# A third attention that makes its scores twice, with the shift put into the queries between

## The chip, the cores and the metric

One core of a Trainium2 chip runs the whole kernel. The metric is the device time of one execution in microseconds; the kernel before takes 1277.92 us, the median of 3 runs (1277.36 to 1278.59). The core's engines are TensorE (PE, with its weight loads as PEld), VectorE (DVE), ScalarE (ACT), GpSimd (POOL) and SyncE (SP, which issues most DMAs). TensorE writes only to PSUM, which here is eight banks of 128 x 512 floats.

## The reference

Everything is float32, for 4 batches of 256 tokens of width 256 and a context `ctx` of the same size. Four layers follow each other:

- L0: two cross attentions to the context (16 heads of 128, one learned key each), and an MLP.
- L1: layer norm, attention of `x` to `ctx` (16 heads of 16, keys masked per batch), MLP.
- L2: attention to the context and `x` together (512 keys, 16 heads of 16, keys masked), MLP.
- L3: grouped-query attention, 32 query heads on 8 key heads of 8, with a full additive mask per batch, then layer norm:

```
scores = einsum("bkgld,bksd->bkgls", q, k) / sqrt(8)
scores = scores + mask                # mask: (B, 1, 256, 256)
attn   = softmax(scores, axis=-1)
out    = einsum("bkgls,bksd->bkgld", attn, v)
y      = layer_norm(out @ Wo + bo + hidden)
```

## The kernel before

The kernel is a list of `Task` objects (L173). A task may have TensorE work (`run`) of one of three shapes, "full" (the whole array), "rows" (contraction of 32, four row groups side by side) and "cols" (32 output columns, four column groups), and posts: work for VectorE, ScalarE, GpSimd or SP once the TensorE work is done. A `Post` that names two engines leaves the choice to the planner. Tiles come from rings: `takes` waits for a free tile, `gives` returns it. `PS` is the ring of eight PSUM banks, `EE` holds weights and MLP activations, `QK` queries and keys, `EQ` (8 tiles) scores and saved sums, `M3` the third attention's mask.

The order of the work is written out by hand as a list of task numbers, `ORDER` (L1841). `plan` (L1754) walks it with a cost for every task and post, picks each free post's engine, and the kernel is issued in that order; every engine then works strictly in its order. A tuple in `ORDER` is two "rows" tasks of different `pair` (row groups 0, 1 and 2, 3) issued interleaved, so that four matmuls run at once; a "rows" task alone keeps half of the row groups idle for the same time. `pe` and `turn` (transpose, a matmul with the identity) and all engine calls pass through `Pinned` (L126), which is why the profile shows L134 nearly everywhere.

The batches go through the layers after L0 one after the other, but the order mixes them: while one is in an MLP, another is in an attention. Before about 700 us only L0 runs.

The third attention (`attention`, L364, with key 3) fetches the mask by SP, makes queries (four copies, one for each group of heads, the rest of the 32 rows zeroed) and keys, and then runs `unit8` (L579) twice per batch, for 16 heads each. For each of four head groups `j`, and for two pairs, `scores` makes 256 x 256 scores with queries in partitions; `least` (VectorE) adds the mask, negates, writes the sum to an `eq` tile and its minimum to `nm`; `exps` (ScalarE) takes the exponential with `nm` as bias; `turns` (TensorE) transposes the weights, since the product with the values needs keys in partitions; the copy to an `e` tile is VectorE's or ScalarE's; `weighted` multiplies with the values, which carry a column of ones for the sum. `ending` (L525) turns the result, divides, and turns it back. At the end of the layer the projection makes its two halves (`part`, L793) in one PSUM bank, `half` adds each to `X`, and `closing` (L923) normalizes and sends it out.

Attentions one and two (`unit16`, L670) make their scores twice already. First with queries in partitions, only for the maxima, which `most` writes negated into a column of a zeroed `shift` tile; that tile is turned (one tile for each of two head groups) and added to the queries, in rows that no head uses (`SHIFT`), opposite a row of ones in the keys. The second scores come out with keys in partitions and less their maxima, so ScalarE takes the exponential straight from PSUM with no turn behind it. Their mask goes with the key and so into the keys (`plus`) or the bias. `open_late` (L1619) makes the tiles of these layers when L0 is done.

Of the kernel before, what the change touches and what calls it, by code (L numbers as in the profile page):

```python
# [51 lines left out]
def kernel(ctx: ExitStack, tc: tile.TileContext, a: dict, out: bass.AP):  # L52
# [60 lines left out]
    SHIFT, HIDDEN = (16, 0), (17, 1)  # L113

# [81 lines left out]
    tasks, stage = [], 0  # L196
# [6 lines left out]
    QK, VV, EQ, OT, XO, M3, HIDES, PLUS, RAW = (Ring([]) for _ in range(9))  # L203
    PO = [Ring([None, None]) for _ in range(2)]
    SHIFTS = [Ring([]), Ring([])]
# [114 lines left out]
    class Layer:  # L320
# [17 lines left out]
        def fill(self):  # L338
# [6 lines left out]
            self.bkx = bk if key == 3 else late_tile([P, 2, 2], f"bkx{key}")  # L345
            for g in range(nh):
                if key == 3:
                    ge.tensor_scalar(self.bqx[:, :, g], self.bq, self.selq[:, g : g + 1], None, ALU.mult)
                else:
# [3 lines left out]
                    )  # L353
            if key != 3:
# [5 lines left out]

                self.hide = late_tile([P, B * S // P], f"hide{key}")
                ge.tensor_scalar(self.hide, self.raw, 0.0, HIDE, ALU.is_equal, ALU.mult)

    def attention(L, b, after, hTs, dst, dst_after, weights_at, before):  # L364
# [13 lines left out]
        if key == 3:  # L378
# [3 lines left out]
            masks = Task(b, None, 0, None, before, takes=[(M3, st, "m")], posts=[Post(("SP",), 100, fetch)], lag=4.0)  # L382
        else:
# [34 lines left out]
        def keys(t, after, q, give):  # L418
# [12 lines left out]
            if key == 3:  # L431
                posts = [affine(lambda: q["kx"](), lambda: u["pt"][2][:, :S], None, lambda: L.bkx[:, t : t + 1], gives)]
                return Task(b, "full", 0.864, run, after, takes=[(PS, u, "pt")], posts=posts)
# [65 lines left out]
        qs, with_mask, use_v = [], [], [[] for _ in L.sources]  # L499
        for t in range(2):  # L500
            q = {"shift": {}}
            q["qm"] = lambda q=q: q["qk"][2][:, : nh * S].rearrange("p (g s) -> p g s", g=nh)
            if key == 3:
                q["kx"] = lambda q=q: q["qk"][2][:, nh * S : nh * S + S]
            else:
                q["kx"] = lambda q=q: q["qk"][2][:, nh * S : nh * S + 2 * NK].rearrange("p (g s) -> p g s", g=2)
            qs.append(q)
# [71 lines left out]
        def unit8(t, q):  # L579
            u = {}  # L580
            S_tasks, V_tasks = [], []
            for j in range(4):
                turned, Ss = [], []
                grab = Task(
                    b, None, 0, None, S_tasks or ready[t] + [masks], behind=vs_taken,
                    takes=[(EE, u, j)] + ([(PO[1], u, "pm"), (PS, u, "po")] if j == 0 else []),
                )
                for pair in range(2):
                    v = {}

                    def scores(j=j, pair=pair, v=v):
                        for qt in range(2):
                            for i in range(2):
# [3 lines left out]
                                    q["qm"]()[r, j, qt * P : (qt + 1) * P], q["kx"]()[r, :], True, True,  # L597
# [3 lines left out]
                    def least(e, i, v=v):  # L601

                        v["nm", i] = sm.tile([P, 2], F32, tag="nm3", name="nm3", bufs=10)
                        for qt in range(2):
                            ve.tensor_tensor_reduce(
                                v["eq", i][2][:, qt, :], v[i][2][:, qt * S : (qt + 1) * S], st["m"][2][:, qt, :],
                                -1.0, BIG, ALU.add, ALU.min, accum_out=v["nm", i][:, qt : qt + 1],
                            )

                    takes = [(PS, v, 0), (PS, v, 1), (EQ, v, ("eq", 0)), (EQ, v, ("eq", 1))]  # L610
                    ts = Task(
                        b, "rows", 0.857, scores, [grab], takes=takes, pair=pair,
                        posts=[
                            Post(("DVE",), 690, lambda e, i=i, least=least: least(e, i), gives=[(PS, v, i)])
                            for i in range(2)
                        ],
                    )
                    Ss.append(ts)
                    for i in range(2):
                        def exps(e, i=i, v=v):  # L620
                            for qt in range(2):
                                to = v["eq", i][2][:, qt, :]
                                se.activation(to, to, AF.Exp, bias=v["nm", i][:, qt : qt + 1], scale=-1.0)

                        def turns(i=i, v=v):
                            for kc in range(2):
# [1425 lines left out]
```

## Time and profile before

| | |
|---|---|
| runs | 1277.36, 1277.92, 1278.59 us |
| profiled execution | 1278.34 us; span 1276.4 us, TensorE clock 0.998 |
| TensorE | 1259.7 us busy, 8907 matmul records |
| VectorE, ScalarE, GpSimd | 833.5, 702.2, 348.7 us busy |
| transposes of `eq` tiles | 624 records of 128x128, 512 of them weights of the third attention |
| score matmuls, 32x256 | 1536 records, two to a matmul, 512 of them in the third attention |
| exponentials of `eq` (ScalarE) | 256, 107.8 us |
| first and last of them | start at 1023.8 and 1261.7 us |

In a group's line stand the line, the engine, the operation, out<-in by the program's names, partitions x elements, the count, then busy time and mean duration, then idle time of the engine before it and what ended it. In the table of stretches each row is a window, its length, then busy time and instruction count of PE, PEld, DVE, ACT and POOL, the granted clock, the DMA share and GB/s. A timeline row has start, duration, engine, line, operation, names, shapes and count. A matmul's duration holds its way through the array, so rows overlap; the pitch is the difference of starts.

### The profile page before, as it was taken

The numbers are of one execution on the slowest core, as the hardware profiler recorded it, in microseconds if no ns is written. First come the engines' busy times: TensorE is split into PE (matmuls) and PEld (weight loads), VectorE is DVE, ScalarE is ACT, GpSimd is POOL, SyncE is SP. The second block draws the span as 40 slices with busy tenths as digits, with TensorE's granted clock in tenths as the row PEclk, the third lists the DMA queues.
The fourth block names the chain that finished last, engine by engine and source line by source line (L and its number), as shares of the span: only waits on it lengthen the run. The fifth ranks groups of instructions, "written<-read, shape, count | busy, mean of one in ns | idle before, by whom it ended". The sixth has DMA issues, their size and how long they took to land.

```text
span 1276.4 us, 23614 instructions
## 1 busy us (share of the span) xinstructions
PE 1259.7 (99%) x8907; PEld 1040.6 (82%) x8907; DVE 833.5 (65%) x2312; ACT 702.2 (55%) x1689; POOL 348.7 (27%) x570
## 2 busy tenths in 40 slices
PE   8999999999999999999999999999999999999997
PEld 4888898999898988899899877768677677677775
DVE  4856656566767566566565358585375587668798
ACT  3554544444545545554544345454535686678896
POOL 7831601414334214151123433121120201002001
PEclk9999999999999999999999999999999999999999
DMA  7010010101101002001020411000000000000000
GB/s 246 18 50 2 33 51 22 62 1 33 51 17 42 26 17 67 1 17 34 1 73 7 149 39 52 2 2 10 1 5 2 1 2 10 1 2 2 18 6 22
DMA packets 25633, 38.08 MB, mean 30 GB/s; under 512 B 2244, under 2 KB 16086, under 8 KB 25392
## 3 DMA queue, kind: packets, MB, share of 16 engines
q1 hardware_dynamic: 24640, 35.56, 8.6%
q0 software_dynamic: 608, 0.76, 0.5%
q8 instruction: 70, 1.15, 0.3%
q14 instruction: 43, 0.35, 0.1%
q10 hardware_dynamic: 272, 0.26, 0.1%
HBM read 35.52 MB, written 1.05 MB: 29 GB/s over the span
## 4 chain that ended last, share of the span: by engine, by line
PE 93%; DVE 3%; POOL 1%; issue 1%; DMA 1%; ACT 0%; SPq 0%; DVEq 0%; POOLq 0%
PE ps_pj L134 25%; PE ps_o L134 23%; PE ps_s L134 23%; PE ps_et L134 22%; DMA craw<-in_ctx_dram 1%; DVE E L134 1%; DVE X L134 1%; POOL f L134 0%; POOL sc L134 0%; DVE nm L134 0%; DVE e L134 0%; DVE eq L134 0%; ACT E L134 0%; SPq L134 0%; POOL cT L134 0%
## 5 line engine op out<-in xcount | busy, mean ns | idle before, releaser
L134 ACT ACTIVATE eq<-eq,nm 128x256 f32<-128x256 f32 x256 | 107.8, 507 | 4.4 <-DVE nm L134 4.2
L134 POOL TENSOR_TENSOR sc<-cT 128x256 f32<-128x256 f32 x62 | 45.3, 731 | 229.8 <-ACT cT L134 202.8
L134 DVE TENSOR_SCALAR E<-E,rinv 128x257 f32<-128x257 f32 x256 | 100.6, 456 | 2.3
L134 PE MATMUL ps_o<-qk 32*128 32x256 f32 (+1 forms) x284 | 79.6, 449 | 0.0
L134 PE MATMUL ps_s<-qk 32*128 32x256 f32 (+1 forms) x272 | 76.2, 461 | 0.0
L134 PE MATMUL ps_pj<-qk 32*128 32x256 f32 (+1 forms) x246 | 70.8, 458 | 0.0
L134 POOL TENSOR_TENSOR X<-X,rowbc 128x256 f32<-128x256 f32 x56 | 40.0, 739 | 97.4 <-PE ps_et L134 49.2
L134 PE MATMUL ps_et<-qk 32*128 32x256 f32 (+1 forms) x222 | 64.9, 448 | 0.0
L134 POOL TENSOR_SCALAR mv<-mv 128x2 f32<-128x2 f32 (+1 forms) x32 | 7.2, 225 | 190.2 <-DVE mv L134 190.0
L134 PE MATMUL ps_o<-eq,qk 32*128 32x256 f32 x224 | 52.3, 398 | 0.0
L134 PE MATMUL ps_pj<-eq,qk 32*128 32x256 f32 x196 | 47.7, 398 | 0.0
L134 ACT ACTIVATE E<-ps_s,nm 128x257 f32<-128x257 f32 x69 | 32.7, 476 | 25.6 <-DVE nm L134 25.6
L134 PE MATMUL ps_et<-eq,qk 32*128 32x256 f32 x180 | 44.4, 397 | 0.0
L134 ACT ACTIVATE E<-ps_et,nm 128x257 f32<-128x257 f32 x73 | 34.6, 475 | 17.2 <-DVE nm L134 17.2
L134 PE MATMUL ps_et<-kT,qT 128*128 128x257 f32 x146 | 43.2, 381 | 0.0
L134 DVE TENSOR_REDUCE nm<-ps_et 128x1 f32<-128x257 f32 x73 | 30.6, 420 | 19.2 <-PE ps_et L134 18.4
L134 PEld LDWEIGHTS ps_o<-qk 32*128 32x128 f32 x284 | 38.3, 184 | 5.8 <-issue 2.3
L134 POOL TENSOR_SCALAR plus<-hide_r,rowof,bkx 128x256 f32<-128x256 f32 x32 | 17.6, 554 | 91.6 <-DVE qk L134 91.2
L134 PE MATMUL ps_s<-eq,qk 32*128 32x256 f32 x168 | 42.2, 398 | 0.0
L134 DVE TENSOR_REDUCE shift<-ps_s 128x1 f32<-128x512 f32 (+1 forms) x54 | 36.8, 684 | 7.5 <-PE ps_s L134 2.7
L134 DVE TENSOR_TENSOR X<-ps_pj,X 128x128 f32<-128x128 f32 (+2 forms) x86 | 25.3, 305 | 23.7 <-PE ps_pj L134 22.4
L134 PE MATMUL ps_o<-eT,V 128*128 128x256 f32 x160 | 40.8, 379 | 0.0
(591 smaller groups left out, 4027.4 us busy)
## 6 DMA issues: line engine op xcount, KB each, us to landing
wk<-in_L_xattn_wk_dram SPq DMA_DIRECT2D x8, 512.0 KB, 3.5
wv<-in_L_xattn_wv_dram SPq DMA_DIRECT2D x8, 512.0 KB, 3.8
wq<-in_L_xattn_wq_dram SPq DMA_DIRECT2D x8, 512.0 KB, 5.0
wo<-in_L_xattn_wo_dram SPq DMA_DIRECT2D x8, 512.0 KB, 3.8
bvb<-in_bv_dram SPq DMA_DIRECT2D x8, 256.0 KB, 5.3
bvl<-in_cols_dram SPq DMA_DIRECT2D x8, 256.0 KB, 5.6
f<-in_L_xattn_w_fc_dram SPq DMA_DIRECT2D x2, 1024.0 KB, 5.0
f<-in_L_xattn_mlp_w_dram SPq DMA_DIRECT2D x2, 1024.0 KB, 5.1
```

The source lines that it names most:

```text
L134: return lambda *args, **more: tc.keep_in_program_order(f(*args, **more))
```

## The change

The third attention takes the form of the other two. Its first scores serve only for `least`, which writes the negated maximum of scores plus mask into one column of a shift tile; the masked scores themselves go to a tile that nobody reads. One shift tile serves all four head groups: group `j` uses row `SHIFT8[j]` of each 32, a row that is zero in that group's queries. The keys are kept in two forms, one with ones in rows 24 to 26 (for groups 0 to 2) and one with ones in row 0 (for group 3). The tile is turned once (two transposes), and four `scalar_tensor_tensor` on VectorE put the shift into the queries in place. The second scores come with keys in partitions, for two head groups and one half of the keys at a time. The mask, which depends on query and key, is turned once per batch and added to them: for half of the row groups VectorE adds it from PSUM into the `e` tile; for the other half ScalarE copies the scores there and GpSimd adds the mask in place. ScalarE then takes the exponential in place. The turns of the weights and their copies are gone.

Besides: attentions one and two use one shift tile for both head groups, so one turn, and put the shift into the queries in place instead of a third tile; queries and keys come free after the second scores, not after the last product with the values; `EQ` has 4 tiles; the last projection uses a PSUM bank for each half; `ORDER` is another list, for the new set of tasks, all stages included.

```diff
 SHIFT, HIDDEN = (16, 0), (17, 1)
+SHIFT8 = (24, 25, 26, 0)
...
+        if key == 3:
+            self.ones, self.selk = late_tile([P, 2], "ones3"), late_tile([P, 2], "selk3")
+            r = [rowof[:, c : c + 1] for c in SHIFT8]
+            ge.tensor_tensor(self.ones[:, 0:1], r[0], r[1], ALU.add)
+            ge.tensor_tensor(self.ones[:, 0:1], self.ones[:, 0:1], r[2], ALU.add)
+            ge.tensor_copy(self.ones[:, 1:2], r[3])
+            ge.tensor_scalar(self.selk, self.ones, -1.0, 1.0, ALU.mult, ALU.add)
+            for v in range(2):
+                ge.tensor_scalar(
+                    self.bkx[:, :, v], bk, self.selk[:, v : v + 1], self.ones[:, v : v + 1], ALU.mult, ALU.add
+                )
...
+            self.picks = late_tile([P, 2], f"picks{key}")
+            for g in range(2):
+                ge.tensor_tensor(
+                    self.picks[:, g : g + 1], rowof[:, SHIFT[g] : SHIFT[g] + 1], rowof[:, HIDDEN[g] : HIDDEN[g] + 1],
+                    ALU.add,
+                )
...
+        def turned():
+            for kc in range(2):
+                for qt in range(2):
+                    turn(
+                        um["pt"][2][:, kc * S + qt * P : kc * S + (qt + 1) * P],
+                        st["m"][2][:, qt, kc * P : (kc + 1) * P],
+                    )
+
+        mask_turned = Task(
+            b, "full", 0.436, turned, [masks], takes=[(PS, um, "pt"), (MT, st, "mt")],
+            posts=[
+                copied(
+                    lambda: st["mt"][2].rearrange("p k q -> p (k q)"), lambda: um["pt"][2], 512, [(PS, um, "pt")]
+                )
+            ],
+        )
...
+            posts = [
+                affine(
+                    lambda v=v: q["kx"]()[:, v, :], lambda: u["pt"][2][:, :S], lambda v=v: L.selk[:, v : v + 1],
+                    lambda v=v: L.bkx[:, t, v : v + 1], gives if v else [],
+                )
+                for v in range(2)
+            ]
...
+        u = {"e": {}}
+        Ms = []
+        grab = Task(b, None, 0, None, ready[t] + [masks], takes=[(SHIFT8S, q["shift"], 0)])
         for j in range(4):
...
+                def maxima(j=j, pair=pair, v=v):
                     for qt in range(2):
...
-                def least(e, i, v=v):
-
-                    v["nm", i] = sm.tile([P, 2], F32, tag="nm3", name="nm3", bufs=10)
+                def least(e, i, j=j, pair=pair, v=v):
+                    at = 64 * pair + 32 * i + SHIFT8[j]
                     for qt in range(2):
                         ve.tensor_tensor_reduce(
-                            v["eq", i][2][:, qt, :], v[i][2][:, qt * S : (qt + 1) * S], st["m"][2][:, qt, :],
-                            -1.0, BIG, ALU.add, ALU.min, accum_out=v["nm", i][:, qt : qt + 1],
+                            unread[0], v[i][2][:, qt * S : (qt + 1) * S], st["m"][2][:, qt, :],
+                            -1.0, BIG, ALU.add, ALU.min, accum_out=q["shift"][0][2][:, qt, at : at + 1],
                         )
 
-                takes = [(PS, v, 0), (PS, v, 1), (EQ, v, ("eq", 0)), (EQ, v, ("eq", 1))]
+                Ms.append(
+                    Task(
+                        b, "rows", 0.857, maxima, [grab], takes=[(PS, v, 0), (PS, v, 1)], pair=pair,
+                        posts=[
+                            Post(("DVE",), 690, lambda e, i=i, least=least: least(e, i), gives=[(PS, v, i)])
+                            for i in range(2)
+                        ],
+                    )
+                )
+        used_m.extend(Ms)
+        v = {}
+
+        def turns(v=v):
+            for qt in range(2):
+                turn(v["pt"][2][:, qt * P : (qt + 1) * P], q["shift"][0][2][:, qt, :])
+
+        def shift(e, j, v=v):
+            qm = q["qm"]()[:, j, :]
+            ve.scalar_tensor_tensor(
+                qm, v["pt"][2][:, :S], rowof[:, SHIFT8[j] : SHIFT8[j] + 1], qm, ALU.mult, ALU.add
+            )
+
+        shifted = Task(
+            b, "full", 0.218, turns, Ms, takes=[(PS, v, "pt")],
+            posts=[
+                Post(("DVE",), 400, lambda e, j=j: shift(e, j), gives=[(PS, v, "pt")] if j == 3 else [])
+                for j in range(4)
+            ],
+            gives=[(SHIFT8S, q["shift"], 0)],
+        )
...
+        for n, (r, kc) in enumerate(((0, 0), (0, 1), (1, 0), (1, 1))):
+            Xs = []
+            grab = Task(
+                b, None, 0, None, [shifted, mask_turned], behind=vs_taken,
+                takes=[(EE, u["e"], n)] + ([(PO[1], u, "pm"), (PS, u, "po")] if n == 0 else []),
+            )
+            for pair in range(2):
+                v = {}
+
+                def weights(r=r, kc=kc, pair=pair, v=v):
+                    for g in range(2):
+                        for i in range(2):
+                            rows = slice(64 * pair + 32 * i, 64 * pair + 32 * i + 32)
+                            j = 2 * r + g
+                            pe(
+                                v[i][2][:, g * S : (g + 1) * S], q["kx"]()[rows, j // 3, kc * P : (kc + 1) * P],
+                                q["qm"]()[rows, j, :], True, True,
+                            )
+                        yield
+
+                def part(i, n=n, pair=pair):
+                    return u["e"][n][2][:, 4 * pair + 2 * i : 4 * pair + 2 * i + 2, :]
+
+                def mask_of(kc=kc):
+                    return st["mt"][2][:, kc, :].rearrange("p (o q) -> p o q", o=1).to_broadcast([P, 2, S])
+
+                def masked(e, v=v, part=part, mask_of=mask_of):
+                    ve.tensor_tensor(part(0), v[0][2].rearrange("p (g q) -> p g q", g=2), mask_of(), ALU.add)
+
+                def unmasked(e, v=v, part=part):
+                    se.copy(part(1).rearrange("p g q -> p (g q)"), v[1][2])
+
+                def masked_there(e, part=part, mask_of=mask_of):
+                    ge.tensor_tensor(part(1), part(1), mask_of(), ALU.add)
+
+                def exps(e, i, part=part):
+                    to = part(i).rearrange("p g q -> p (g q)")
+                    se.activation(to, to, AF.Exp)
+
                 ts = Task(
-                    b, "rows", 0.857, scores, [grab], takes=takes, pair=pair,
+                    b, "rows", 0.857, weights, [grab], takes=[(PS, v, 0), (PS, v, 1)], pair=pair,
                     posts=[
-                        Post(("DVE",), 690, lambda e, i=i, least=least: least(e, i), gives=[(PS, v, i)])
-                        for i in range(2)
+                        Post(("DVE",), 600, masked, gives=[(PS, v, 0)]),
+                        Post(("ACT",), 477, unmasked, gives=[(PS, v, 1)]),
                     ],
                 )
...
+                all_W.append(ts)
+                tm = Task(b, None, 0, None, [ts], posts=[Post(("POOL",), 1430, masked_there)])
+                all_W.append(tm)
+                for i, t_ in enumerate((ts, tm)):
+                    Xs.append(
+                        Task(b, None, 0, None, [t_], posts=[Post(("ACT",), 560, lambda e, i=i, exps=exps: exps(e, i), EXP)])
                     )
...
+            def weighted(n=n, r=r, kc=kc):
+                for g in range(2):
                     for s in range(4):
-                        at = 16 + 32 * (4 * t + s) - 16 * j2
+                        at = 16 + 32 * (4 * t + s) - 16 * g
                         pe(
                             u["po"][2][32 * s : 32 * s + 32, r * S : (r + 1) * S],
-                            st["V0"][2][:, kc, at : at + 32], u[j][2][:, 2 * s + kc, :],
-                            j == 0 and kc == 0, j2 == 1 and kc == 1, skip_group_check=True,
+                            st["V0"][2][:, kc, at : at + 32], u["e"][n][2][:, 2 * s + g, :],
+                            n == 0 and g == 0, g == 1 and kc == 1, skip_group_check=True,
                         )
 
...
+                    b, "cols", 0.887, weighted, Xs + vs + V_tasks[-1:], takes=[(EQ, u, "c")] if n == 3 else [],
+                    posts=[saved(u)] if n == 3 else [], gives=[(EE, u["e"], n)],
...
+        used_mt.extend(all_W)
+        Task(b, None, 0, None, behind=all_W, gives=[(QK, q, "qk")])
...
+        v = {}
+
+        def turns(v=v):
+            for qt in range(2):
+                turn(v["pt"][2][:, qt * P : (qt + 1) * P], q["shift"][0][2][:, qt, :])
+
+        def shift(e, g, v=v):
+            qm = q["qm"]()[:, g, :]
+            ve.scalar_tensor_tensor(qm, v["pt"][2][:, :S], L.picks[:, g : g + 1], qm, ALU.mult, ALU.add)
+
+        shifted = Task(
+            b, "full", 0.218, turns, Ms, takes=[(PS, v, "pt")],
+            posts=[
+                Post(("DVE",), 400, lambda e, g=g: shift(e, g), gives=[(PS, v, "pt")] if g else []) for g in range(2)
+            ],
+            gives=[(SHIFTS, q["shift"], 0)],
+        )
...
-                                q["qx"][2][r, g, :], True, True,
+                                q["qm"]()[r, g, :], True, True,
...
-                    w["pt"][2][:, qt * D : (qt + 1) * D], st["oT"][2][:, k, qt * P : (qt + 1) * P], L.w[3][:, k, :],
-                    k == 0 and qt == 0, k == 1, skip_group_check=True,
+                    w[qt][2][:, :D], st["oT"][2][:, k, qt * P : (qt + 1) * P], L.w[3][:, k, :], k == 0, k == 1,
+                    skip_group_check=True,
                 )
...
         first = Task(
-            b, "full", 0.864, lambda: part(0, (0, 1)), ends[:1] + dst_after, takes=[(PS, w, "pt")]
+            b, "full", 0.864, lambda: part(0, (0, 1)), ends[:1] + dst_after, takes=[(PS, w, 0), (PS, w, 1)]
...
-                    posts=[Post(("DVE",), 340, lambda e, qt=qt: half(e, qt), gives=[(PS, w, "pt")] if qt else [])],
+                    posts=[Post(("DVE",), 340, lambda e, qt=qt: half(e, qt), gives=[(PS, w, qt)])],
...
-    (EQ, 8, [P, 2, S], "eq"),
+    (EQ, 4, [P, 2, S], "eq"),
...
+    (MT, 2, [P, 2, S], "m3t"),
...
+    (SHIFTS, 3, [P, 2, P], "shift"),
+    (SHIFT8S, 2, [P, 2, P], "shift8"),
...
+    unread.append(late_tile([P, S], "unread"))
+    for t in SHIFT8S.tiles:
         ge.memset(t, 0.0)
-        ge.memset(t.rearrange("p a (s c) -> p a s c", c=32)[:, :, :, HIDDEN[i % 2]], -1.0)
-        SHIFTS[i % 2].tiles.append(t)
+    for t in SHIFTS.tiles:
+        ge.memset(t, 0.0)
+        for c in HIDDEN:
+            ge.memset(t.rearrange("p a (s c) -> p a s c", c=32)[:, :, :, c], -1.0)
...
 ORDER = (
-    47, 12, 9, 54, 48, 49, 13, 11, 2, 64, 23, 3, 24, 51, 61, 29, 10, 22, 63, 30, 25, 66, 31, 28, 226, 52, 14, 227,
...
+    47, 9, 29, 13, 12, 48, 51, 49, 2, 54, 23, 30, 11, 3, 64, 24, 10, 22, 63, 62, 52, 61, 31, 25, 66, 33, 36, 226,
...
```

## The prediction

> **What bounds the kernel now.** I read the page first: busy shares, the span in 40 slices, and the chain that ended last.
>
> ```profile
> PE 1259.7 (99%) x8907; PEld 1040.6 (82%) x8907; DVE 833.5 (65%) x2312; ACT 702.2 (55%) x1689; POOL 348.7 (27%) x570
> PE   8999999999999999999999999999999999999997
> ...
> DVE  4856656566767566566565358585375587668798
> ACT  3554544444545545554544345454535686678896
> ...
> PEclk9999999999999999999999999999999999999999
> ...
> PE 93%; DVE 3%; POOL 1%; issue 1%; DMA 1%; ACT 0%; SPq 0%; DVEq 0%; POOLq 0%
> ```
>
> TensorE works without a pause at full clock, and the chain is TensorE for 93%. DVE and ACT are half busy for 30 slices, then eight or nine tenths. The table of stretches shows how close they come at the end:
>
> ```profile
> 700.00:1000.00 300.00, 299.96 (x2439) 227.56 (x2438) 180.60 (x395) 143.92 (x264) 70.09 (x130) 1.00 0.10 28
> 1000.00:1100.00 100.00, 100.00 (x933) 73.44 (x932) 75.90 (x251) 71.69 (x149) 10.84 (x18) 1.00 0.01 4
> 1200.00:1250.00 50.00, 49.97 (x511) 38.15 (x511) 46.41 (x203) 45.53 (x107) 3.00 (x6) 1.00 0.04 12
> 1250.00:1277.00 27.00, 18.70 (x193) 12.73 (x191) 21.82 (x81) 14.75 (x35) 3.58 (x8) 0.87 0.07 25
> ```
>
> Columns are PE, PEld, DVE, ACT, POOL. From 1200 to 1250, where the last attention runs almost alone, VectorE is busy 46.4 of 50 and ScalarE 45.5; GpSimd 3.0. So a saving on TensorE is worth its full size except at the end, where a shift of work to VectorE can cost time.
>
> Last, prices: groups by shape, and the timeline for the pitch at which instructions follow each other (a group's mean includes overlap).
>
> ```profile
> L134 ACT ACTIVATE eq<-eq,nm 128x256 f32<-128x256 f32 x256 | 107.8, 507 | 4.4 <-DVE nm L134 4.2
> L134 DVE CUSTOM_DVE_ANT_0 eq<-ps_o,m 128x256 f32<-128x256 f32 x74 | 28.1, 420 | 2.7 <-PE ps_pj L134 1.2 <-PE ps_s L134 0.8 <-PE ps_et L134 0.3
> L134 DVE TENSOR_TENSOR u<-ps_pj,bvb 128x512 f32<-128x512 f32 x27 | 18.6, 689 | 14.2 <-PE ps_pj L134 14.2
> L134 POOL TENSOR_TENSOR bvb<-bvb,bvl 128x512 f32<-128x512 f32 x7 | 9.0, 1285 | 0.0
> ```
>
> ```profile
> 1242.71 0.48 PE L134 MATMUL ps_o<-qk 32*128 32x256 f32 x1
> ...
> 1243.79 1.07 PE L134 MATMUL ps_pj<-e,V 128*32 128x256 f32 x16
> 1244.79 0.66 PE L134 MATMUL ps_s<-ident,eq 128*128 128x128 f32 x4
> ...
> 1246.15 0.60 PE L134 MATMUL ps_pj<-ident,eq 128*128 128x128 f32 x4
> 1246.59 0.60 PE L134 MATMUL ps_et<-ident,eq 128*128 128x128 f32 x4
> ...
> 1269.68 0.87 PE L134 MATMUL ps_s<-w3o,oT 128*128 128x256 f32 x2 [0.52 <-DVE X L134]
> ```
>
> Four transposes take 0.44 (1246.15 to 1246.59). A pair of score tasks, eight matmuls on all four row groups, takes 1.08 from 1242.71 to 1243.79, 0.21 of it the change of shape behind it (below): 0.86.
>
> **The change, part by part: TensorE.** The last attention has 8 units (4 batches, 2 halves).
> - Removed: 16 tasks of four transposes per unit, 128 x 0.436 = 55.8 us.
> - Added: 8 score tasks per unit, 64 in all (256 to 320 row-shaped tasks). The order list says how they pair: before 127 pairs and 2 single tasks, 129 slots; after 156 pairs and 8 single, 164 slots. 35 x 0.857 = 30.0 us.
> - The shift tiles: attentions one and two turn one tile per unit instead of two (16 x 0.218 = -3.5); the third turns one (+1.7), and 4 masks (+1.7): 0.
> - Changes of shape. Taking the list of before task by task gives 108 row, 89 full and 57 column runs, exactly the 254 runs in the trace. The new list gives 132, 83 and 66. By the timeline's medians a run's end costs 0.21 after rows, 0.14 after columns, 0.20 after full: +24 x 0.21 + 9 x 0.14 - 6 x 0.20 = +5.1 us.
> - The last projection gets a bank per half, so its second half no longer waits for the addition of the first: 0.52 in the fence, another 0.52 in the group of these matmuls; at the very end 0.8 (1268.47 to 1269.68, against a pitch of 0.43). Together -1.3.
>
> Sum on TensorE: -55.8 + 30.0 + 5.1 - 1.3 = -22.0 us.
>
> **The other engines**, by pitches. ScalarE loses 256 exponentials (0.41) and 74 of the 128 copies of turned weights (0.48), and gets 64 copies (0.48) and 128 exponentials of 128x512 (0.57, from the exponentials of the other attentions): -38 us. VectorE loses 54 copies (0.60), gets 64 masked additions (0.61, the row u<-ps_pj,bvb back to back) and 32 shifts (0.39); the shifts of attentions one and two change form (0.33 to 0.39, 32 times): +21. The minima stay. The second form of the keys is 8 small writes on either engine: under 4 us, hidden by half-idle engines before 1200; without cover 4. GpSimd gets 64 additions at 1.29 = 82 us into a stretch where it had 28: room enough. The constants (ones, picks, memsets) are some 30 GpSimd instructions of 0.1 to 0.35 us, under 8 us, while TensorE works through the first MLPs; GpSimd runs 70 of 300 us there. Without that cover, up to 8.
>
> Do the new additions disturb VectorE? In the trace, VectorE instructions with SBUF operands only do stretch beside a GpSimd tensor_tensor: TENSOR_SCALAR 128x257 took 859 ns wholly beside one, 349 beside none. With PSUM input they don't: 128x512 additions 688 against 689, the minima 420 against 420. All new VectorE work reads PSUM: 0 us.
>
> The Trainium skill (GPSIMD Engine Reference, Engine selection) speaks against this split: elementwise additions of two inputs belong on VectorE, GpSimd being about twice as slow. The rows here say 1285 against 689 ns, 1.87 times. By the rule the 64 additions would go to VectorE and cost it 64 x 0.61 = 39 us more in the fullest stretch; by the rows GpSimd is idle there, and I keep the 82 us beside other work.
>
> **Waits.** New: the second scores wait for the shift, minima (0.42), turn (0.22), four shifts (1.6). What stands between in the list covers it: 2.6 to 9.8 us between last maximum and turn in six units, but 2.3 and 1.9 in the last two; then 4.9 to 14, and in the last two 2.1 and 3.2. Behind a late shift TensorE's whole queue waits, then ScalarE's copies. Also new: ScalarE waits for GpSimd's addition (copy 0.59, addition 1.29); copies that free PSUM banks queue behind that exponential, and the roots of norms queue behind additions on GpSimd. The list puts 5.6 us or more between second scores and their use. SP's mask fetches (0.39 each) stay four, behind the same output DMAs. The eq ring halves to 4 tiles, but its largest user, the score tiles, goes; a late tile would cost one save, 0.6.
>
> **The tail.** The last 50 us of TensorE work in the new list hold 14 maxima tasks (four minima each: 1.38), 26 masked additions, 2 shift groups (1.6), 4 quotients (1.3), 6 half additions (0.34), 6 closings (1.4): VectorE 19.3 + 15.6 + 3.2 + 5.2 + 2.0 + 8.4 = 53.7 us. ScalarE has 26 x 0.48 + 59 x 0.57 + some 4 = 50. TensorE's last instruction came 6 us before the end, so these 104 us stand in 56 us of two engines: 93%. The old list's last 50 us: measured 46 + 39 = 85 in 106, 80%. 13 of the 14 maxima stand in 25 us, where VectorE's share comes to 117%. Bounds: no stretch (0), or the old 80% again: 104 / 1.6 = 65, so +9. I take +5: nearest is the 1200 to 1250 row, where 92% was reached with TensorE never waiting, but with work split evenly between the engines, which the new list can't do.
>
> The new order also rearranges the first 700 us without changing its work. Idle there is 8.4, of which 5.9 is the first loads: +-3, taken as 0.
>
> **Sum:** -22.0 + 5 = -17 us on the profiled execution (span 1276.4, 1278.34 with what lies around). The median of the runs, 1277.92, is 0.4 below: 1277.9 - 17 = 1261.
>
> The Trainium skill (Perfetto Trace Analysis, Identifying the Most-Contended Engine) judges TensorE's headroom not by matmul busy time but by weight loads: 82% here, 74% from 1000 on. By that rule only some three quarters of 22 would be real, 16.5, and the sum -11.5, 1266. The rows show no idle TensorE queue except 11 us, so I keep the full size.
>
> **Rivals.**
> 1. *The tail hides everything* (VectorE's surplus of 25 us drains in the next 25): -22, 1256, less with luck in the first part, 1253. Against it: the two gaps of 2 us.
> 2. *VectorE becomes the bound of the last attention*: per unit it has 32 x 0.345 + 8 x 0.61 + 1.6 + 1.3 = 18.8 us, TensorE some 14. If the last three units run at VectorE's pace, +14: 1270. For it: b=1 to 3 mix in the last 75 us; against: ScalarE takes the free choices, and MLP work is mixed in before.
> 3. *Slower: the trip through GpSimd.* Each of the 64 masked halves goes PSUM, ScalarE, GpSimd, ScalarE. If ScalarE's in-order queue blocks on it and banks stay full, up to 1.29 us each comes onto the path, 82 us; over 22/64 = 0.34 us each, it is slower than before; at 0.5, 1288. Against: 5.6 us of cover.
> 4. *The order takes back what the work gives*: the rearranged first 700 us lose 17, and it stays at 1278. Against it: the same tasks at the same prices.
>
> **How the numbers follow.** Forecast (1257 to 1266) 55%, rival 1 13%, rival 2 19%, rival 3 9%, rival 4 4%. A difference under 0.2% (2.6 us) is what a measurement here can't tell. Faster 0.86, same 0.04, slower 0.10. Range: 1253 (rival 1) to 1273 (rival 2 and a little more); the rest is in rivals 3 and 4.
>
> **What would show it.** The changed profile should have 512 fewer 128x128 transposes, 512 more 32x256 records, TensorE busy near 1240, GpSimd near 430, VectorE near 855, ScalarE near 665. A span above 1265 with TensorE idle after 1190, released by DVE, is rival 2; released by ACT or POOL, rival 3. I am wrong if TensorE's busy time falls by less than 15, or if gaps open before 1000.

## The result, and the profile after

The changed kernel takes **1286.64 us** (median of 4 runs, 1286.20 to 1289.82) against 1278.03 for the kernel before beside it: a ratio of 1.0074, interval 1.0059 to 1.0089. It is 8.6 us slower; the forecast was 1261, 17 us faster, with the likeliest mechanism on the wrong side.

The page of the changed kernel: busy time of each engine, slices, chain. (The profiled execution took 1289.82 us, the longest of the four, so its span reads some 3 us long.)

```profile
PE 1265.2 (98%) x8907; PEld 1021.4 (79%) x8907; DVE 871.1 (68%) x2355; ACT 673.6 (52%) x1568; POOL 428.8 (33%) x643
...
DVE  4856567665777566666575467574685787788987
ACT  3554543545545454454453246555535656766875
POOL 7941502413524224421124423121120035115555
PEclk9999999999999999999999999999999999999988
...
PE 91%; DVE 6%; DMA 1%; issue 1%; SPq 0%; ACT 0%; DVEq 0%
```

The side engines' totals moved about as forecast: ScalarE fell by 28.6 us, GpSimd rose by 80.1. TensorE should have fallen by 20 and rose by 5.5, and VectorE has twice the chain's share it had (6% against 3%). The table of stretches says where:

```profile
1000.00:1100.00 100.00, 99.90 (x880) 72.02 (x884) 78.08 (x245) 59.11 (x106) 27.21 (x32) 1.00 0.01 4
1100.00:1200.00 100.00, 99.75 (x1044) 67.37 (x1036) 85.69 (x329) 72.55 (x139) 30.71 (x30) 1.00 0.02 4
1200.00:1250.00 50.00, 47.62 (x500) 28.26 (x493) 45.35 (x174) 37.11 (x72) 28.48 (x26) 0.97 0.01 2
1250.00:1290.00 40.00, 28.62 (x269) 18.15 (x266) 29.89 (x86) 21.82 (x43) 21.71 (x26) 0.82 0.08 27
```

From 1200 on TensorE is no longer full (47.6 of 50; 49.97 before). VectorE is busy 45.4 of 50 there, no more than before, with fewer instructions, 174 against 203. So it is not full by its busy time, and still gets less done. What TensorE waits for between 1000 and 1260 (total, times, longest, in us; the five longest):

```profile
PE ps_o L135 <- DVE shift L135: 0.7, 2, 0.4
PE ps_et L135 <- DVE qk L135: 0.6, 1, 0.6
PE ps_s L135 <- DVE shift L135: 0.3, 1, 0.3
PE ps_et L135 <- DVE shift L135: 0.3, 1, 0.3
PE ps_pj L135 <- DVE shift L135: 0.3, 1, 0.3
```

Every one is VectorE, and they add up to little over 2 us: the loss isn't in recorded gaps. (`DVE shift` is here the accumulator read of a minimum, which writes the shift tile and frees the PSUM bank; only `DVE qk` is the shift's addition to the queries.) It shows when TensorE's time is taken from the start of each run of one shape to the start of the next:

| us | before | after | difference | forecast |
|---|---|---|---|---|
| full runs (89, then 83) | 1052.0 | 1000.2 | -51.8 | -58.3 |
| rows runs (108, then 132) | 136.5 | 196.0 | +59.5 | +35.0 |
| column runs (57, then 66) | 77.1 | 79.4 | +2.3 | +1.3 |

(The forecast by shape is the prediction's sum of -22.0, with its changes of shape put to the run that ends: -55.8 - 1.2 - 1.3; 30.0 + 5.0; 1.3.) The runs are as many as the order list was read to give. The transposes went as priced. The score matmuls take 24.5 us too much: matmuls of a pair start late, and a late start inside a busy array leaves no gap. In 11 places behind 1000 us a score matmul starts over 0.33 us after the one ahead of it and 62 to 64 ns after the end of a minimum on a PSUM bank of its name; with two tiles for the minima (run 1 below) there are 2 such places.

So the minima are late. The group's line says nothing: the same instruction, the same duration (420 ns before).

```profile
L135 DVE CUSTOM_DVE_ANT_0 unread<-ps_s,m 128x256 f32<-128x256 f32 x78 | 32.9, 422 | 7.5 <-PE ps_et L135 1.4 <-ACT e L135 1.1 <-PE ps_o L135 0.5
```

The pitch says it. VectorE's timeline before (start, duration), and then after:

```profile
1149.88 0.42 DVE L134 CUSTOM_DVE_ANT_0 eq<-ps_o,m 128x256 f32<-128x256 f32 x1
1150.22 0.08 DVE L134 DVE_READ_ACCUMULATOR2_ANT nm<- 128x1 f32 x1
1150.22 0.42 DVE L134 CUSTOM_DVE_ANT_0 eq<-ps_o,m 128x256 f32<-128x256 f32 x1
1150.57 0.08 DVE L134 DVE_READ_ACCUMULATOR2_ANT nm<- 128x1 f32 x1
1150.57 0.42 DVE L134 CUSTOM_DVE_ANT_0 eq<-ps_pj,m 128x256 f32<-128x256 f32 x1
```

```profile
1211.41 0.42 DVE L135 CUSTOM_DVE_ANT_0 unread<-ps_et,m 128x256 f32<-128x256 f32 x1
1211.76 0.08 DVE L135 DVE_READ_ACCUMULATOR2_ANT shift<- 128x1 f32 x1
1211.99 0.42 DVE L135 CUSTOM_DVE_ANT_0 unread<-ps_o,m 128x256 f32<-128x256 f32 x1
1212.34 0.08 DVE L135 DVE_READ_ACCUMULATOR2_ANT shift<- 128x1 f32 x1
1212.45 0.42 DVE L135 CUSTOM_DVE_ANT_0 unread<-ps_o,m 128x256 f32<-128x256 f32 x1
1212.80 0.08 DVE L135 DVE_READ_ACCUMULATOR2_ANT shift<- 128x1 f32 x1
1213.03 0.42 DVE L135 CUSTOM_DVE_ANT_0 unread<-ps_s,m 128x256 f32<-128x256 f32 x1
```

Before, a minimum starts 0.345 us after the one ahead, while that one, 0.42 long, still runs. After, it starts only once the one ahead and its accumulator read are over, 0.46 to 0.58 later. Over all pairs under 0.7 us apart (220 before, 202 after) the mean pitch went from 346 to 505 ns; for all 256 minima that would be 256 x 0.16 = 41 us of VectorE in the last 280 us, an estimate. 15 of them show as busy time (871.1 us against 855.7 in run 1 below: the overlap is gone), and some 12 as gaps of 0.04 to 0.15 us before minima, of which the tile's own view puts 1.4 us down to VectorE. The list of the built program's instructions, with the semaphores that each waits for, tells why (before; after):

```
eq_4876,nm_9094<-ps_o,m_4886 128x256
nm_9094 128x1
eq_4876,nm_9094<-ps_o,m_4886 128x256
nm_9094 128x1
eq_4875,nm_9097<-ps_pj,m_4886 128x256 [waits PE_49]

unread,shift_4896<-ps_o,m_4884 128x256 [waits DVE_49]
shift_4896 128x1
unread,shift_4896<-ps_o,m_4884 128x256 [waits DVE_49]
shift_4896 128x1
unread,shift_4896<-ps_pj,m_4884 128x256 [waits DVE_49,PE_49]
```

All minima now write the same tile, the one that nobody reads. Two writes to one tile must keep their order, so 240 of the 256 wait for VectorE's own semaphore; before, 8 did.

The clock has a smaller part in the loss, as its row in the page hints. In the profiled execution TensorE's granted clock was halved for 3.4 us from 1238 and for 6.8 us from 1251.6, while matmuls ran: 16 column matmuls took 1.7 us there against 1.0 right after, 16 score matmuls 2.0 against 1.1. That is 5.1 us of lost clock at most; some 1.9 us of it fall in rows runs and 2.4 in full runs. The other three executions have a mean clock of 0.995, against 0.998 in all four of run 1, so some 4 us each. The kernel before shows a halved clock only behind its last matmul. Of the profiles below, those of runs 2, 3, 4 and 7, in which full-length minima wait for one another, have it during the work too, and those of runs 1, 5, 6, 8 and 9 don't. Run 3 shows that it isn't the loss: two of its executions had a mean clock of 0.998 and took 1285.35 and 1286.94 us, two had 0.995 and took 1285.83 and 1286.08; with two tiles (run 6) the same kernel takes 1267.89. What sets it off was not tested.

### The profile page after: what moved, and what is told of

It reads as the page before. It is cut to its first block, busy times and chain, and to the rows that moved or that the text cites. A ratio compares the mean times of both kernels' runs of the same rounds, so it can differ in the third digit from the quotient of the medians.

```text
span 1288.0 us, 23601 instructions
## 1 busy us (share of the span) xinstructions
PE 1265.2 (98%) x8907; PEld 1021.4 (79%) x8907; DVE 871.1 (68%) x2355; ACT 673.6 (52%) x1568; POOL 428.8 (33%) x643
## 4 chain that ended last, share of the span: by engine, by line
PE 91%; DVE 6%; DMA 1%; issue 1%; SPq 0%; ACT 0%; DVEq 0%
PE ps_et L135 24%; PE ps_pj L135 23%; PE ps_o L135 22%; PE ps_s L135 22%; DVE unread L135 2%; DVE E L135 1%; DMA craw<-in_ctx_dram 1%; DVE e L135 1%; DVE X L135 1%; DVE qk L135 0%; DVE u L135 0%; SPq L135 0%; DVE V L135 0%; DVE shift L135 0%; DVE xo L135 0%
## 5 line engine op out<-in xcount | busy, mean ns | idle before, releaser
L135 PE MATMUL ps_s<-qk 32*128 32x256 f32 (+1 forms) x662 | 159.8, 427 | 0.6 <-DVE shift L135 0.3
L135 PE MATMUL ps_pj<-qk 32*128 32x256 f32 (+1 forms) x604 | 152.6, 429 | 0.4 <-DVE shift L135 0.3
L135 PE MATMUL ps_o<-qk 32*128 32x256 f32 (+1 forms) x554 | 141.1, 429 | 0.8 <-DVE shift L135 0.7
L135 PE MATMUL ps_et<-qk 32*128 32x256 f32 (+1 forms) x484 | 128.4, 428 | 1.1 <-DVE qk L135 0.6
L135 PEld LDWEIGHTS ps_s<-qk 32*128 32x128 f32 x662 | 87.0, 186 | 16.3 <-issue 4.5
L135 POOL TENSOR_TENSOR e<-e,m3t 128x512 f32<-128x512 f32 x50 | 63.3, 1282 | 100.9 <-ACT e L135 97.6
L135 PEld LDWEIGHTS ps_pj<-qk 32*128 32x128 f32 x604 | 82.9, 185 | 17.6 <-issue 7.7
L135 PEld LDWEIGHTS ps_et<-qk 32*128 32x128 f32 x484 | 69.4, 185 | 15.4 <-DVE shift L135 5.0
L135 ACT ACTIVATE e<-e 128x512 f32<-128x512 f32 x100 | 58.2, 631 | 3.9 <-DVE e L135 3.0
L135 DVE TENSOR_TENSOR X<-ps_pj,X 128x128 f32<-128x128 f32 (+2 forms) x72 | 21.7, 311 | 28.6 <-PE ps_pj L135 27.5
L135 PE MATMUL ps_s<-eT,V 128*128 128x256 f32 x156 | 39.9, 379 | 0.0
```

What stands on the lines that cost most here:

```text
L135: return lambda *args, **more: tc.keep_in_program_order(f(*args, **more))
```

## The experiments

Theory A: the single unread tile makes each minimum wait for the one ahead, and that is the loss. Its rivals: the trip through GpSimd, the new order of the first stage (D), and later VectorE's work as such (V). The letters are those of the texts on record, which say what each stands for.

**1. Two tiles in turn.**

```diff
-                                unread[0], v[i][2][:, qt * S : (qt + 1) * S], st["m"][2][:, qt, :],
+                                unread[(2 * i + qt) % len(unread)], v[i][2][:, qt * S : (qt + 1) * S], st["m"][2][:, qt, :],
...
-        unread.append(late_tile([P, S], "unread"))
+        unread.extend(late_tile([P, S], f"unread{i}") for i in range(2))
```

> Edit: the minima of the third attention write their unread scores to two tiles in turn instead of one. Theory A (own waits): in the changed kernel every minimum waits for the one before it on VectorE itself, since all write the same tile; the pitch of the minima is 467 to 580 ns there (mean 505) against 345 before, 256 x 0.16 = 41 us of VectorE time in the last 280 us, and TensorE's score runs wait for it. It expects a pitch near 350 ns and a time of 1259 to 1267 us. Theory B (the trip through GpSimd blocks ScalarE and the PSUM banks): the time stays within 3 us of 1286.6. Theory C (VectorE simply has too much work in the last attention, waits or not): about half of it, 1272 to 1280.

**1268.70 us** (1268.08 to 1268.91), ratio 0.9928, interval 0.9913 to 0.9943: 17.9 us off the changed kernel, and 9.3 faster than the kernel before. It misses A's range by 1.7 at the upper end. Clock and chain, stretches and the minima of this kernel:

```profile
PEclk9999999999999999999999999999999999999999
...
PE 95%; DVE 3%; DMA 1%; ACT 0%; SPq 0%; issue 0%; DVEq 0%
```

```profile
1100.00:1200.00 100.00, 99.92 (x1099) 68.37 (x1094) 85.07 (x352) 76.66 (x149) 36.74 (x36) 1.00 0.02 4
1200.00:1250.00 50.00, 49.28 (x590) 31.60 (x583) 48.87 (x190) 46.83 (x92) 39.12 (x36) 1.00 0.01 2
1250.00:1290.00 40.00, 7.16 (x67) 4.04 (x66) 11.85 (x39) 3.80 (x8) 5.02 (x12) 0.91 0.08 26
```

```profile
1191.63 0.41 DVE L135 CUSTOM_DVE_ANT_0 unread<-ps_o,m 128x256 f32<-128x256 f32 x1
1191.97 0.08 DVE L135 DVE_READ_ACCUMULATOR2_ANT shift<- 128x1 f32 x1
1191.97 0.42 DVE L135 CUSTOM_DVE_ANT_0 unread<-ps_o,m 128x256 f32<-128x256 f32 x1
```

The pitch is 345 again, the chain is TensorE's for 95%, TensorE is full to 1250, and the clock is halved only behind the last matmul. The engines run the same instructions as in the changed kernel, in the same numbers. One added tile of 128 x 256 turns the change from a loss into a gain.

**2. No second tile: the minima write back into their own bank.**

```diff
-                                unread[0], v[i][2][:, qt * S : (qt + 1) * S], st["m"][2][:, qt, :],
+                                v[i][2][:, qt * S : (qt + 1) * S], v[i][2][:, qt * S : (qt + 1) * S], st["m"][2][:, qt, :],
```

> Edit: the minima write their unread scores back into the PSUM bank they read, so that only the second of the two minima of a bank follows one on the same tile. Theory A: if a wait for VectorE's own instruction is what costs, half of the minima lose it and half keep it; mean pitch near 0.41 us, time between the changed kernel and the run with two tiles, 1268 to 1278 us. Theory B: within 3 us of 1286.6. Theory C: as B, or a little faster.

1282.01 us (1281.73 to 1283.50), ratio 1.0033 [1.0021, 1.0046]. A smaller gain than theory A's 1268 to 1278: the first minimum of a bank follows at 350, but the second, which waits for the first, at 541 in the mean, later than the 464 of two that share the SBUF tile. The mean pitch is 474, between the other two, and so is the time.

**3. GpSimd's additions left out.**

```diff
                     def masked_there(e, part=part, mask_of=mask_of):
-                        ge.tensor_tensor(part(1), part(1), mask_of(), ALU.add)
+                        pass
```

> Edit: the 64 additions of the mask on GpSimd are left out, so half of the row groups get no mask and ScalarE takes those exponentials right after its copy. Theory B (the trip through GpSimd): 15 us or more faster than the changed kernel, 1272 or less. Theory A and C: at most 4 us faster, 1283 to 1287, since GpSimd is half idle and the exponential's wait isn't on the path.

1285.95 us (1285.35 to 1286.94): 0.7 from the changed kernel, inside the spread of the runs. The trip through GpSimd is not what costs.

**4. The first stage in the old list's order.**

```diff
-        47, 9, 29, 13, 12, 48, 51, 49, 2, 54, 23, 30, 11, 3, 64, 24, 10, 22, 63, 62, 52, 61, 31, 25, 66, 33, 36, 226,
...
+    ORDER = repaired(ORDER)
```

(The places of the first stage's tasks are filled with the same tasks in the sequence of the old list; a task whose forerunners aren't done is put behind them.)

> Edit: within the new order list the tasks of the first layer follow each other as in the old list (their numbers are the same in both); where one would come before a task that it needs, the next free one goes first. Theory D (the new order of the first 700 us costs something): 3 us faster than the changed kernel, 1283.5, since by the matmuls' columns the changed kernel has done 3.1 us less work after 700 us than the one before. Theory A alone: no difference, 1286.6 within 1.5.

1291.77 us (1291.48 to 1292.84), 5.1 slower than the changed kernel. The new list's first part isn't the loss, but the run says no more than that: the old sequence doesn't fit the new list (TensorE waits 2.5 us at 675.9 and 1.1 at 692.1 for GpSimd).

The next three ask what holds the two-tile kernel at 1268.7 instead of 1261.

**5. Two tiles, VectorE's mask additions left out.**

```diff
+                    def unread_mask(e, v=v, part=part):
+                        se.activation(part(0).rearrange("p g q -> p (g q)"), v[0][2], AF.Exp)
...
+                        if i == 0:
+                            return
...
-                            Post(("DVE",), 600, masked, gives=[(PS, v, 0)]),
+                            Post(("ACT",), 600, unread_mask, EXP, gives=[(PS, v, 0)]),
```

> This kernel has two tiles for the unread scores, as the one measured at 1268.7 us, and leaves out the 64 additions of the mask on VectorE: for those row groups ScalarE's exponential reads the PSUM bank and writes the weights, so the weights of half the row groups are not masked; ScalarE has no instruction more or less, VectorE has 64 x .689 = 44 us less, nearly all of it after 1000 us. Theory V (what is left above the forecast is VectorE, full in the last stretch: 85.1 us busy in 1100 to 1200 and 48.9 of 50 in 1200 to 1250; the runs in which maxima and weights of the last attention follow one another take 11.4 us over their matmuls where 18 runs x .212 would be 3.8): those 7.6 us go, and the time is 1259 to 1264. Theory G (the trip through GpSimd holds the end): that trip is still there, and the time stays within 1.5 us of 1268.7. Theory O (the rest is lost before 1000 us or in the very last projections, where this kernel changes nothing): also within 1.5 us of 1268.7.

**1277.50 us** (1277.19 to 1277.90): 8.8 *slower* than with the additions. No theory expected that. The edit moved a second thing: both banks of a pair are now freed by ScalarE, in one queue with exponentials that wait for GpSimd. What ScalarE waits for between 1000 and 1260 in this kernel:

```profile
ACT e L135 <- PE ps_et L135: 18.0, 11, 7.0
ACT e L135 <- PE ps_s L135: 15.6, 10, 5.8
ACT e L135 <- PE ps_pj L135: 14.8, 15, 5.9
ACT e L135 <- POOL e L135: 6.2, 6, 1.8
```

In the two-tile kernel the wait for GpSimd isn't among the ten longest of that stretch, the last of which is 1.2 us. And a third: the planner, which gives free posts to an engine by its load, moved 20 copies and affine writes from ScalarE to VectorE, so that VectorE's busy time fell by 27 us only (855.7 to 828.4), not by 44. Which of these makes the 8.8 is argued at best; no run takes them apart. As a test of theory V the run is void.

**6. Two tiles, GpSimd's additions left out** (the edit of 3).

> Two tiles for the unread scores, and the 64 additions of the mask on GpSimd left out (the other half of the row groups is not masked; copies and exponentials stay). Theory G: with VectorE freed of its own wait the trip through GpSimd, 1.28 us for an addition and GpSimd busy for 39 us of 1200 to 1250, is what ends last; without it the time is 1261 to 1266. Theory V: VectorE is as full as before, GpSimd's work lay beside it; 1267.2 to 1270.

1267.89 us (1267.57 to 1268.12), 0.8 less. With GpSimd busy 1.6 of the 50 us (39.1 with the additions), nothing else moves:

```profile
1200.00:1250.00 50.00, 49.28 (x594) 31.59 (x587) 48.05 (x192) 46.81 (x92) 1.58 (x4) 1.00 0.01 3
```

**7. One tile, VectorE's mask additions left out** (the edit of 5 in the changed kernel).

> The changed kernel with its one tile for the unread scores, VectorE's wait on itself thus kept, and VectorE's 64 additions of the mask left out as in the first kernel of this call. Theory A1 (the wait costs nothing but VectorE's time, 256 x .16 = 41 us, in a stretch where VectorE has none to spare): 44 us less of other work pay for it, and the time is 1266 to 1273. Theory A2 (the wait holds up the PSUM banks of the row pairs directly, each by its own delay, however much room VectorE has): most of the 17.9 us remain, 1279 to 1286.

1294.45 us (1293.58 to 1295.31). Read against run 5, which differs from it only in the tiles, the wait costs 17.0 us, nearly as much as with the additions (17.9). VectorE has less to do in both (25 and 27 us less busy, after what the planner moved to it; 36.5 of 50 in run 5), and still the wait costs its price. That speaks for the pace at which a burst of minima frees its banks, and against VectorE's total. A2 was the right side, by the wrong number, since neither theory knew of run 5's loss.

**8 and 9. Minima over half the keys, with two tiles and with one.** Here the bank is freed by the same engine in the same order, and only the length of the instruction changes.

```diff
-                                unread[(2 * i + qt) % len(unread)], v[i][2][:, qt * S : (qt + 1) * S], st["m"][2][:, qt, :],
+                                unread[(2 * i + qt) % len(unread)][:, :P], v[i][2][:, qt * S : qt * S + P], st["m"][2][:, qt, :P],
```

> Two tiles for the unread scores, and each of the 256 minima is taken over the first 128 keys only (the other 128 scores of each query are left out of the maxima; the weights are made from all of them, so a query's shift can be short of its largest score). Every bank is freed by the same engines in the same order as in the kernel at 1268.7 us; the pitch of two minima falls from 345 to about 345 - 128 x 1.04 = 212 ns, 256 x .133 = 34 us of VectorE. Theory V (what is left over the forecast is TensorE waiting in rows for banks that VectorE has still to read: the 18 runs of maxima and weights mixed take 11.4 us over their matmuls where .212 each would be 3.8): the mixed runs fall to below 6 us, and the time is 1260 to 1264.5. Theory O (those waits are set by the order, the PSUM banks held for other engines, or lie before and behind this stage): 1266.5 to 1269.5.

> The changed kernel with its one tile for the unread scores, its 256 minima over the first 128 keys only, as in the other kernel of this call. VectorE's wait on itself stays: the pitch of two minima should fall from 467 (580 across banks, 505 in the mean) by the same 133 ns, to some 335, 450 and 372 in the mean. Theory P (only the pitch counts, .114 us of the end for each ns of it, from 1268.7 at 347, 1282.0 at 474 and 1286.6 at 505): 1270 to 1274. Theory W (the wait itself is the harm, whatever the instruction's length, because what is queued behind it stands still): 1280 to 1286.

With two tiles **1267.27** (1266.23 to 1269.09); with one **1268.66** (1268.42 to 1269.13). The second settles P against W: the wait is still there, in 240 of the 256 minima, but with a mean pitch of 371 the kernel is as fast as the one without the wait at 347. So the wait does harm by the pitch that comes with it. P's straight line is wrong, though (it gave 1270 to 1274), and the first run refutes V: with VectorE idle for 7 of 50 us the time falls by 1.4 only.

```profile
1100.00:1200.00 100.00, 99.93 (x1106) 68.50 (x1106) 70.03 (x351) 77.12 (x149) 36.55 (x36) 1.00 0.02 5
1200.00:1250.00 50.00, 49.13 (x612) 31.38 (x608) 43.05 (x198) 47.75 (x95) 40.22 (x39) 1.00 0.01 4
```

The doses together. The last column is the sum of rival 2 with the measured pitch put in for its 0.345: VectorE per unit 7.8 + 32 x pitch, TensorE 14, the difference for the last three units, on 1278 - 22:

| minima | mean pitch, ns | time, us | rival 2's sum |
|---|---|---|---|
| half keys, two tiles | 230 | 1267.3 | 1259 |
| two tiles | 347 | 1268.7 | 1271 |
| half keys, one tile | 371 | 1268.7 | 1273 |
| into their bank | 474 | 1282.0 | 1283 |
| one tile (the change) | 505 | 1286.6 | 1286 |

Up to 371 ns something else sets a floor at 1267 to 1269; at 474 and 505 the time is longer, and rival 2's sum comes within 1 us of it. That is two points, put together with the results known and with some halved clock in both, so it describes and proves nothing. It does not hold where VectorE's 64 additions are left out: with 4.9 us less per unit it gives 1272 for run 7 (pitch 511, measured 1294.45) and 1256 for run 5 (pitch 349, measured 1277.50), where ScalarE frees the banks.

## Why the prediction was wrong

- **The step that failed is "The minima stay"**, in the working for the other engines. It kept the pitch of the kernel before, 0.345, and so the 1.38 us for a task of four minima and VectorE's +21. The instruction did stay (420 and 422 ns). Its output didn't: from a ring of `EQ` tiles to a single tile, and with it came a wait for the instruction ahead. The diff showed this: `unread[0]` in place of `v["eq", i]`. The part on waits listed the new waits between engines and left out those of an engine for itself. Measured: 505 ns in the mean, some 41 us of VectorE by the estimate above, and 17.9 us of the time (run 1), up to some 4 of them by way of the halved clock. Of the 25.6 us between forecast and result that leaves 7.7, the two-tile kernel's distance from 1261.
- **The removal was priced right.** In the two-tile kernel the full runs take 996.0 us, 56.0 less than before, where 58.3 was forecast.
- **The added scores were priced right as work and too low as time**: 164 slots x 0.857 and 132 runs x 0.21 are 168.3 us; two tiles take 178.7, one tile 196.0. By the same count the kernel before was 3.3 over. So stalls in the rows runs, over those of before, are 24.4 us with one tile (1.9 at most from the halved clock) and 7.1 with two. With two tiles TensorE's busy time is 14.4 us below before, where the forecast had 20 and called itself wrong under 15.
- **The tail** was taken as +5, with bounds 0 and +9, for VectorE's surplus. With two tiles, TensorE ends 12.3 us earlier than before (1258.25 against 1270.55), and 2.2 us more follow its end (8.05 against 5.88). The 7.1 of stalls and these 2.2 are 9.3: the upper bound, not the +5. And the term's reason is doubtful: run 8 takes VectorE's surplus away and gains 1.4.
- **Other engines.** VectorE +21: +22.2 with two tiles, +37.6 with one. GpSimd +82: +80.1. ScalarE -38 (its terms add up to -37): -28.6. Nothing hung on the last.
- **No contention for VectorE work that reads PSUM**: right. In the changed kernel the minima take 421.9 ns wholly beside a GpSimd addition and 422.6 beside none.
- **The waits for the shift** came where they were put, in the last units, and are small: of the rows above only `DVE qk` is one, 0.6 us, and its matmul starts 0.98 us after the one ahead. The `DVE shift` rows, 1.6 us, are banks that a minimum frees.
- **Rival 2** (VectorE becomes the bound of the last attention) named the engine. What was to show it did: a span above 1265 and TensorE's waits after 1190 ended by VectorE. With 505 ns instead of 345 its sum gives 1286 instead of 1270. Its mechanism, a VectorE with more work per unit than TensorE, isn't shown by that: runs 5 and 7 don't fit the sum, and in run 8 VectorE works less and next to nothing is gained. The price of the minimum was the one number in it that was not questioned.
- **Rival 3** (the trip through GpSimd) fell: 0.7 and 0.8 us (runs 3 and 6). The Trainium skill's rule in GPSIMD Engine Reference, Engine selection, would have moved these additions to VectorE, the engine that turned out to be late; here one takes 1282 ns on GpSimd and 683 on VectorE, 1.88 times, in line with the page, but no run tried the move.
- **Rival 4 and the first 700 us.** By 700 us TensorE had done 3.1 us less work than before, by the columns of its matmuls: the edge of the +-3 allowed. Run 4 doesn't improve on it.

What stays open: why the two-tile kernel stands at 1268.7 and not at 1261. It is not GpSimd's additions (run 6) and for 1.4 us at most the length of the minima (run 8). More than half of the stalls left (some 6 of 10.4 us, with the 3.3 that were there before) lie in ten runs of the last 60 us that mix first and second scores. The longest holds 3.3 us; in it one matmul starts 0.9 us after the one ahead, just behind the addition of the shift to the queries. The forecast put waits of that kind there, but no run takes them apart.

## What to carry to other kernels

When a change redirects an output, look who wrote that tile last: a scratch tile that nobody reads still orders its writers, and here a second one cost only room. Price an instruction by its pitch in the stream, with the waits that the new stream gives it, and not by its duration, which stays the same. And compare instruction counts with busy time in a stretch: an engine that is hardly less busy and does fewer instructions may be held, and the pitch of like instructions tells.

## What the runs showed of the hardware

The price of VectorE's wait for itself, by what a minimum waits for (median pitch of neighbours, ns; number of them):

| waits for | one tile | two tiles | half keys, one tile |
|---|---|---|---|
| nothing of VectorE | | 345 (15) | |
| VectorE alone | 466 (134) | 345 (119) | 334 (134) |
| VectorE and one engine | 576 (51) | 345 (51) | 443 (50) |
| VectorE and two engines | 605 (17) | 344 (14) | 472 (14) |

With two tiles 225 minima still wait for VectorE's semaphore, but for the minimum before the last or something older, and it costs nothing. A wait for the instruction directly ahead costs 121 ns; each further semaphore then adds to it, 110 for the first and some 30 for the second, though in the kernel before and with two tiles the same semaphores are free. The traces show where the difference lies: further semaphores are waited for by an instruction of their own ahead of the minimum. In the changed kernel one of these (21 ns) starts at 1211.88, after the accumulator read has ended at 1211.84, and the minimum follows at 1211.99. With two tiles one starts at 1192.09, while the minimum of 1191.97 to 1192.38 still runs.

The Trainium skill (VectorE: DVE Perf Modes, The DRAIN you can't avoid) says that the pipeline empties behind every VectorE instruction before the next one starts, unless that one isn't held, and reports eight copies to take the same time with a semaphore after each as with one at the end: "the semaphore costs nothing extra here". The runs here differ where the next instruction isn't held otherwise. Unheld, a minimum of 420 ns is followed at 345; held by the one ahead, at 466 to 605. In this kernel that was 17.9 us.
